# A four-layer transformer sandwich: factors summed in the transfers, the last batch by query halves, due times by kind of work

## The chip, the core and the metric

The kernel runs on one core of one Trainium2 chip. The core has TensorE (PE, matrix products, with its own queue of weight loads, PEld), VectorE (DVE), ScalarE (ACT), GpSimd (POOL) and SyncE (SP, which only issues transfers here). Each engine works through its own queue strictly in order; semaphores hold an instruction back until what it needs is there. Sixteen DMA engines move data for all queues. The metric is the device time of one execution in microseconds (us); lower is better.

## The reference, cut to what matters

The input is 8 batches of 512 tokens by 512 features, all float32. Four layers follow each other, each as `x = x + layernorm(f(layernorm(x)))`:

```
attn0:  w = softmax(x^T x)          # over features: a 512x512 Gram matrix
        f = w-weighted sum of the feature rows
ffn0:   f = sum_r (x @ factors[r]) / sqrt(8) + bias      # 8 factors of 512x512
attn1:  h = norm_scale * x / rms(x) * split_scale
        q = h Wq^T (8 heads of 64), k, v = h Wk^T, h Wv^T (2 groups)
        f = x + softmax(q k^T / 8) v  Wo^T
ffn1:   g = (x gate_w^T) * gate_s;  u = (x up_w^T) * up_s     # 1408 inner features
        f = ((silu(g) * u) down_w^T) * down_s                 # weights are -1, 0, 1
```

Because ffn0 is linear in the factors, one product with the sum of the eight factors serves for all of them.

## The kernel before, in words

**Tiles.** A batch is four token tiles of 128 rows (NT = 4); features are four blocks of 128 (KT = 4). The inner width of ffn1 is eleven tiles (NI = 11), held in two buffers hd0 and hd1 (six and five tiles, `CUTS`). Head pairs in attn1 are four (NPAIR). A 512-column float32 product is recorded as two passes, so a product over four blocks shows as eight matmul records.

**The order of work is planned.** The code of a stage does not issue instructions: it calls `add(engine, duration, function, reads, writes, ...)`, which records an operation with its data dependences, the buffers it needs and a due time `rec.prio`. `Recorder.issue` (L108) then plays a clock for each engine. Again and again it takes for each engine the operations whose inputs are there, keeps those that can start within `slack` of the earliest, picks the one with the smallest due time, and issues it. The result is a fixed order for each engine's queue. The planner gives every transfer on SP a latency of 2.6 us and the weight loads on POOL 3.0 us; a change of TensorE's tiling mode costs 0.1 us in the plan and a change of ScalarE's function table 1.3 us. Four buffers "e" hold exponentials, two "z" hold branch outputs, four "ws" attention weights, four "wgu" gate and up weights; PSUM has five banks "f" and three "g". A tag's buffers are handed on when their last reader is done.

**Due times before.** A stage's due time is batch number + a fixed offset + a span times a step: `ATTN0`, `FFN0`, `ATTN1`, `FFN1` at L1149 to L1152. One unit is one batch. So attn1 of batch b, due from b + 0.55 to b + 1.15, and ffn1, from b + 1.68, lie among the next batches' first layers, and the planner mixes them.

**Start of the kernel.** `load_fixed` (L388): for each block kt, SP loads factor 0 straight into `fsum` (L394) and the other seven into staging slots in hd0 and hd1 (L397), and DVE adds each (L401). The x of batches 0 and 1 is due earlier still (L1131). `look_at_low_bits` (L420) loads gate, up and down weights once more as raw words into the same slots, 33 pieces, and ORs them on DVE into a z buffer (L442), to see whether any low bit is set; ffn1 uses the single-pass format F32R, and a full-precision run of everything follows if the flag says so. POOL loads the down weights `wd` (L372) as soon as its queue is free.

**Layers.** Layer norms take their statistics on DVE (L495, L500), the reciprocal root on POOL (L504, L511) and the normalisation on DVE (L519); the residual add is POOL's (L537). Attn0 (L607) transposes the normalised x (L587), forms the Gram rows (L626), softmaxes them (L551 to L575) and applies them (L655). Ffn0 (L666) multiplies by fsum (L677). Attn1 (L698) forms keys, values and queries (L809, L820, L838). Then for each head pair i and query half u it forms scores for two query tiles (L869, 64-row tiling), transposes (L900, 64-row) and mixes with the values (L931, 64-column). When all pairs are done, four token tiles are projected (L959). Ffn1 (L1006) normalises all four tiles of x, splits them into a high and a low part `hl` (L990 on ACT, L999 on DVE), and for each inner tile loads the weights on POOL (L372), forms gate and up products for all 512 tokens (L1032, 8 records each), and combines them (L1052 on ACT, L1062 and L1071 on DVE). The down product (L1100) follows for each token tile, then the scale (L1113), the layer norm, the residual add and the store (L1123).

Of the kernel before, what the change touches and what calls it, by code (L numbers as in the profile page):

```python
# [12 lines left out]
I32 = mybir.dt.int32  # L13
# [40 lines left out]
class Recorder:  # L54
# [53 lines left out]
    def issue(self, places, slack=0.1):  # L108
# [26 lines left out]
        while left:  # L135
            best = None
            for e, ops in ready.items():
                able = [(s, op.prio, op.n, op) for op in ops if (s := start(op)) is not None]
                if not able:
                    continue  # L140
                first = min(able)[0]
                pick = min((p, n, s, op) for s, p, n, op in able if s <= first + slack)
                if best is None or (pick[2], pick[1]) < best[:2]:
                    best = (pick[2], pick[1], pick[3])
# [93 lines left out]
def layers(  # L238
# [99 lines left out]


# [48 lines left out]
    def load_fixed():  # L388
        rec.prio = 0.15

        slots = staging()
        for kt in range(KT):
            rec.prio = 0.15 + 0.01 * kt
            load(fsum, factors[0, ts(kt, P), :], part=kt, view=lambda t, kt=kt: t[:, kt, :])  # L394
            for r in range(1, R):
                f, j = next(slots)
                load(f, factors[r, ts(kt, P), :], part=j, view=lambda t, j=j: t[:, j, :])  # L397

                def go(f=f, j=j, kt=kt):
                    d = fsum.t[:, kt, :]  # L400
                    nc.vector.tensor_tensor(d, d, f.t[:, j, :], ALU.add)  # L401

                add("DVE", 0.69, go, reads=[(f, j)], writes=[(fsum, kt)])
        load(bias_bc, ffn_bias.partition_broadcast(P))
        rec.prio = 0.3
# [7 lines left out]
        rec.prio = 0.95  # L413
# [6 lines left out]
    def look_at_low_bits():  # L420

        low, most, total = Buf("z"), Buf("s1"), Buf("f")
        rec.prio = 1.0
        bits = lambda: low.t[:, :].bitcast(I32)
        add("DVE", 0.3, lambda: nc.vector.memset(bits(), 0), writes=[low])
        slots = staging()
        pieces = [(w, c) for w in (gate_t, up_t, down_t) for c in range(NI)]
        for n, (w, c) in enumerate(pieces):
            rec.prio = 1.0 + 0.01 * n
            raw, j = next(slots)  # L430
            if w is down_t:
                load(raw, w[ts(c, P), :], part=j, view=lambda t, j=j: t[:, j, :])
            else:
                load(
                    raw,
                    w[:, ts(c, P)].rearrange("(k p) n -> p k n", p=P),
                    part=j,
                    view=lambda t, j=j: blocks(t[:, j, :]),
                )

            def gather(raw=raw, j=j):
                nc.vector.tensor_tensor(  # L442
                    bits(), bits(), raw.t[:, j, :].bitcast(I32), ALU.bitwise_or
                )

            add("DVE", 0.69, gather, reads=[(raw, j)], writes=[low])
# [83 lines left out]
    def add_layernorm(xt, src, us=0.55):  # L530

        y = buf_of(src) if buf_of(src).tag == "z" else Buf("z")
        layernorm(whole(y), src, us)
        add(
            "POOL",
            1.27,
            lambda: nc.gpsimd.tensor_tensor(ap(xt), ap(xt), y.t[:, :], ALU.add),  # L537
# [69 lines left out]
    def stage_attn0(x, at, span):  # L607
        xn, xnT, wT = Buf("big"), Buf("big"), Buf("big")
        rec.prio = at
# [7 lines left out]
        for i in range(KT):  # L617
            rec.prio = at + span * (0.1 + 0.1 * i)
# [30 lines left out]
        for t in range(NT):  # L649
            rec.prio = at + span * (0.5 + 0.1 * t)  # L650
# [15 lines left out]
    def stage_ffn0(x, at, span):  # L666
        for t in range(NT):
            rec.prio = at + span * 0.2 * t
# [29 lines left out]
    def stage_attn1(x, at, span):  # L698
# [3 lines left out]
        for t in range(NT):  # L702
            rec.prio = at + span * 0.05 * t
# [97 lines left out]
        rec.prio = at + span * 0.2  # L801
# [28 lines left out]

        for i in range(NPAIR):
            rec.prio = at + span * (0.22 + 0.13 * i)
# [13 lines left out]
            asked = mm(pq, 3.43, queries, [wq, hT], room=[qT])  # L846
# [10 lines left out]
        wos = []  # L857
        for i in range(NPAIR):
            for u in range(2):
                aT = Buf("big")  # L860
                for s in (2 * u, 2 * u + 1):
                    rec.prio = at + span * (0.25 + 0.13 * i + 0.03 * s)
                    es = [Buf("e") for _ in range(G)]
                    scs = [Buf("f") for _ in range(G)]

                    def scores(i=i, s=s, scs=scs):
                        for g in range(G):
                            gp = ts(g, DH)
                            nc.tensor.matmul(  # L869
                                scs[g].t[:, :],  # L870
                                qT.t[gp, i, ts(s, P)],
                                kT.t[gp, :],
                                start=True,
                                stop=True,
                            )

                    add(
                        "PE",
                        0.87,
                        scores,  # L880
                        reads=[(qT, (i, u)), kT],
                        writes=scs,
                        room=[*es, aT],
                        state="64x128",
                    )
                    for g in range(G):
                        softmax_row(scs[g], es[g])


                    pts = [Buf("f") for _ in range(2)]  # L890

                    def halves(b):
                        return b.t[:, :].rearrange("p (c q) -> p c q", q=DH)

                    def transposes(es=es, pts=pts):
                        for g in range(G):
                            for t in range(NT):
                                for hf in range(2):
                                    hp = ts(hf, DH)
                                    nc.tensor.transpose(  # L900
                                        halves(pts[hf])[:, g * NT + t, :],
                                        es[g].t[hp, ts(t, P)],
                                        ident[hp, hp],
                                    )

                    add("PE", 0.56, transposes, reads=es, writes=pts, room=[aT], state="64x128")
                    for hf in range(2):

                        def place(hf=hf, s=s, aT=aT, pts=pts):
                            lo = s % 2 * P + hf * DH  # L910
                            copy = nc.scalar.copy
                            copy(columns_of(aT)[:, :, lo : lo + DH], halves(pts[hf]))  # L912

                        add(
                            "ACT",
                            0.6,
                            place,
                            reads=[pts[hf]],
                            writes=[(aT, 2 * s + hf)],
                        )  # L920
                rec.prio = at + span * (0.29 + 0.13 * i + 0.03 * s)
                po = Buf("f")

                def columns_of(b):
                    return flat(b.t).rearrange("p (c q) -> p c q", q=2 * P)

                def values_of(aT=aT, po=po):
                    for t in range(NT):
                        for g in range(G):
                            gp = ts(g, DH)  # L930
                            nc.tensor.matmul(  # L931
                                po.t[gp, : 2 * P],
                                v.t[:, t * P + g * DH : t * P + (g + 1) * DH],
                                columns_of(aT)[:, g * NT + t, :],
                                start=(t == 0),
                                stop=(t == NT - 1),
                            )

                attended = mm(po, 1.75, values_of, [aT, v], state="128x64")

                add(
                    "ACT",
                    0.4,
                    lambda i=i, u=u, po=po: nc.scalar.copy(
                        qT.t[:, i, ts(u, 2 * P)], po.t[:, : 2 * P]
                    ),
                    reads=[po],
                    writes=[(qT, (i, u))],
                )
            wos.append(Buf("ws"))  # L950
            load(wos[i], wo_t[ts(i, P), :], view=flat, after=[asked])

        for t in range(NT):
            rec.prio = at + span * (0.8 + 0.03 * t)
# [25 lines left out]
            add_layernorm(whole(x[t]), whole(z))  # L980
        return last
# [24 lines left out]
    def stage_ffn1(x, b, at, span, after):  # L1006
        PASS = 0.23 if split else 0.86
        xs = [Buf("hl") for _ in range(1 + split)]
        for t in range(NT):
            rec.prio = at + span * 0.01 * t  # L1010
            xn = Buf("row")
            mv, rstd = moments(whole(x[t]))
            normalize(whole(xn), whole(x[t]), mv, rstd, room=xs)
# [187 lines left out]
```

## Time and profile before

| | |
|---|---|
| median of 3 runs | 1568.37 us (1568.25 to 1568.81) |
| the profiled execution's own time | 1568.29 us |
| its span, first to last instruction | 1566.5 us |
| PE busy | 1503.5 us, 96% |
| PE busy in 0–117, 117–1467, 1467–1567 us | 91.6 of 117, 1333.3 of 1350, 78.7 of 100 us |
| DVE busy | 1080.4 us, 69% |
| ACT, POOL busy | 702.2 and 566.4 us |
| mean granted clock of PE | 0.988 |
| moved by DMA | 105.87 MB |

The profile is one execution, taken by the hardware profiler. "Busy" of PE counts overlapping matmuls once, and includes the draining between tiling modes; it says that PE had something in its pipe, not that it ran at its peak. In lists of instructions a line reads: start, duration, engine, source line, operation, tiles out<-in, shape, count, and in brackets the idle time before it and what ended it. In lists of groups, the numbers are total, mean of one in ns, and idle time before with its releasers.

### The profile page before, as it was taken

What the parts mean: (1) busy time and instruction counts of PE and PEld (TensorE: products, weight loads), DVE (VectorE), ACT (ScalarE), POOL (GpSimd) and SP (SyncE); (2) the same over time, 40 slices, a digit from 0 to 9 for tenths busy, and PEclk for the clock granted to TensorE, in tenths of its full rate; (3) what the DMA queues carried; (4) which work ended last, traced back from release to release, by engine and by line L of the source; (5) the groups of instructions that cost most, each with busy time, mean ns of one, the idle gap of its engine ahead of it and who ended that gap; (6) DMA issues with size and microseconds to landing.
All of it is one profiled execution on the core that took longest, in us unless ns stands there. A gap on an engine that the chain in (4) does not pass through costs nothing.

```text
span 1566.5 us, 21966 instructions
## 1 busy us (share of the span) xinstructions
PE 1503.5 (96%) x7986; PEld 923.6 (59%) x7986; DVE 1080.4 (69%) x2226; ACT 702.2 (45%) x1448; POOL 566.4 (36%) x869
## 2 busy tenths in 40 slices
PE   6799999999999999999999999999999999999896
PEld 3354456665666646665566656666566665666485
DVE  6898865679557794587845788458865678557734
ACT  2045546541376324763257523575236742277221
POOL 3614341137410473115721257103651036411532
PEclk9899999999999999999999999999999999999999
DMA  9540043212331124302142132411233102330170
GB/s 346 165 155 1 1 101 75 44 52 54 74 75 28 41 57 91 62 28 72 30 89 53 40 75 42 88 35 48 61 61 81 21 34 61 74 75 14 35 132 31
DMA packets 152471, 105.87 MB, mean 68 GB/s; under 512 B 6945, under 2 KB 132897, under 8 KB 152353
## 3 DMA queue, kind: packets, MB, share of 16 engines
q0 software_dynamic: 94512, 49.03, 16.5%
q1 hardware_dynamic: 57840, 55.34, 11.3%
q8 instruction: 65, 1.06, 0.3%
q14 instruction: 54, 0.43, 0.1%
HBM read 95.96 MB, written 8.39 MB: 67 GB/s over the span
## 4 chain that ended last, share of the span: by engine, by line
PE 81%; DVE 9%; POOL 5%; DMA 2%; issue 2%; ACT 1%; SPq 0%; POOLq 0%; ACTq 0%; DVEq 0%
PE g L1032 21%; PE g L1100 11%; PE f L869 8%; PE f L931 7%; PE f L838 7%; PE f L677 7%; PE f L900 5%; PE f L959 4%; PE f L587 3%; PE f L626 3%; DVE row L519 3%; POOL rstd L511 2%; DVE st L495 2%; PE f L820 2%; PE f L809 2%
## 5 line engine op out<-in xcount | busy, mean ns | idle before, releaser
L1032 PE MATMUL g<-hl,wgu 128*128 128x512 f32 x1408 | 350.3, 400 | 0.7 <-ACT hl L990 0.7
L551 DVE TENSOR_REDUCE s<-f 128x1 f32<-128x512 f32 x288 | 186.5, 683 | 185.3 <-PE f L869 171.3
L1032 PEld LDWEIGHTS g<-hl,wgu 128*128 128x128 f32 x1408 | 258.9, 189 | 81.5 <-issue 18.4
L504 POOL TENSOR_SCALAR ve<-mv 128x1 f32<-128x1 f32 x224 | 71.1, 317 | 523.0 <-DVE mv L500 509.0
L558 ACT ACTIVATE e<-f,s 128x512 f32<-128x512 f32 x288 | 195.8, 688 | 87.0 <-DVE s L551 81.2
L537 POOL TENSOR_TENSOR x<-x,z 128x512 f32<-128x512 f32 x128 | 169.5, 1324 | 61.6 <-DVE z L519 53.1
L1100 PE MATMUL g<-wd,hl 128*128 128x512 f32 x704 | 180.7, 406 | 3.2 <-DVE hl L999 3.2
L912 ACT COPY big<-f 128x512 f32<-128x512 f32 x256 | 134.4, 597 | 60.1 <-PE f L900 59.2
L1100 PEld LDWEIGHTS g<-wd,hl 128*128 128x128 f32 x704 | 129.0, 189 | 45.0 <-issue 11.5
L372 POOL DMA_DIRECT2D wgu<-in_up_t x88 | 67.3, 765 | 235.9 <-PE g L1032 235.8
L575 DVE TENSOR_SCALAR e<-e,s 128x512 f32<-128x512 f32 x288 | 144.0, 500 | 10.2
L511 POOL TENSOR_TENSOR rstd<-ve,mhalf 128x1 f32<-128x1 f32 x224 | 143.1, 639 | 18.1
L869 PE MATMUL f<-kv,big 64*128 64x512 f32 x512 | 138.6, 628 | 0.0
L1062 DVE SCALAR_TENSOR_TENSOR sig<-g,gs,sig 128x512 f32<-128x512 f32 x88 | 65.8, 748 | 98.4 <-ACT sig L1052 98.4
L931 PE MATMUL f<-big,kv 128*64 128x256 f32 x1024 | 124.6, 385 | 0.0
L372 POOL DMA_DIRECT2D wgu<-in_gate_t x88 | 68.7, 781 | 140.3 <-PE g L1032 137.1
L677 PE MATMUL f<-fsum,rT 128*128 128x512 f32 x256 | 116.7, 604 | 0.7 <-ACT rT L591 0.7
L959 PE MATMUL f<-ws,big 128*128 128x512 f32 x256 | 114.9, 594 | 0.6 <-ACT big L794 0.6
L838 PE MATMUL f<-big,ws 128*128 128x512 f32 x256 | 114.1, 594 | 0.0
L655 PE MATMUL f<-big,big 128*128 128x512 f32 x256 | 112.3, 594 | 0.7 <-ACT big L591 0.7
L931 PEld LDWEIGHTS f<-big,kv 128*64 128x64 f32 x1024 | 67.8, 136 | 71.8 <-ACT big L912 13.8
L900 PEld LDWEIGHTS f<-ident,e 64*128 64x128 f32 x2048 | 71.7, 139 | 43.7 <-issue 32.0
(81 smaller groups left out, 1971.3 us busy)
## 6 DMA issues: line engine op xcount, KB each, us to landing
wgu<-in_gate_t POOLq DMA_DIRECT2D x88, 256.0 KB, 3.3
wgu<-in_up_t POOLq DMA_DIRECT2D x88, 256.0 KB, 3.4
x<-in_x SPq DMA_DIRECT2D x32, 256.0 KB, 2.7
ws<-in_wq_t SPq DMA_DIRECT2D x32, 256.0 KB, 3.3
ws<-in_wo_t SPq DMA_DIRECT2D x32, 256.0 KB, 2.6
out<-x SPq DMA_DIRECT2D x32, 256.0 KB, 2.0
hd<-in_factors SPq DMA_DIRECT2D x28, 256.0 KB, 5.4
wd<-in_down_t POOLq DMA_DIRECT2D x11, 256.0 KB, 8.1
```

Of the source, the lines that this page charges most:

```text
L511: lambda: nc.gpsimd.tensor_tensor(rstd.t[:, :], ve.t[:, :], mhalf, ALU.pow),
L537: lambda: nc.gpsimd.tensor_tensor(ap(xt), ap(xt), y.t[:, :], ALU.add),
L551: lambda: nc.vector.tensor_reduce(nmax.t[:, :], sc.t[:, :], AX.X, ALU.max, negate=True),
L558: lambda: nc.scalar.activation(e.t[:, :], sc.t[:, :], AF.Exp, bias=nmax.t[:, :], accum_out=tot.t[:, :]),
L677: nc.tensor.matmul(po.t[:, :], xnT.t[:, kt, :], fsum.t[:, kt, :], start=(kt == 0), stop=(kt == KT - 1),)
L838: nc.tensor.matmul(pq.t[:, :], wq.t[:, kt, :], hT.t[:, kt, :], start=(kt == 0), stop=(kt == KT - 1),)
L869: nc.tensor.matmul(scs[g].t[:, :], qT.t[gp, i, ts(s, P)], kT.t[gp, :], start=True, stop=True,)
L900: nc.tensor.transpose(halves(pts[hf])[:, g * NT + t, :], es[g].t[hp, ts(t, P)], ident[hp, hp],)
L931: nc.tensor.matmul(po.t[gp, : 2 * P], v.t[:, t * P + g * DH : t * P + (g + 1) * DH], columns_of(aT)[:, g * NT + t, :], start=(t == 0), sto ...
L959: nc.tensor.matmul(po.t[:, :], qT.t[:, i, ts(t, P)], flat(wos[i].t), start=(i == 0), stop=(i == NPAIR - 1),)
L1032: nc.tensor.matmul(bank.t[:, :], w.t[:, kt, :], d.t[:, kt, :], start=(n == 0), stop=(n == KT * len(xs) - 1),)
L1100: nc.tensor.matmul(po.t[:, :], ap(o)[:, it - lo, :], wd.t[:, it, :], start=(it == 0 and k == 0), stop=(it == NI - 1 and k == len(ops) - 1),)
```

## The change

It has four parts.

1. *Factors.* The seven further factors of each block are no longer loaded into staging slots and added on DVE. POOL issues transfers with `accum_op=add` straight onto `fsum`. Each writes the same part of fsum as the one before, so it waits for that one's landing.
2. *Low bits.* The collector `low` is a staging slot instead of a z buffer, cleared on POOL instead of DVE, and the stage is due later (1.41 on, instead of 1.0 on).
3. *Last batch* (`EARLY = (-1,)`). Attn1 loops over query halves outside and head pairs inside, and projects a half's two token tiles when its four pairs are done. Ffn1 takes the first four inner tiles (`FEW`) for tokens 0–1, then for tokens 2–3 (each loads its weights anew, and products are 256 columns wide), and the other seven for all tokens. The residual adds of this batch's last two layers are on DVE. In every batch the down products are now recorded as after all gate and up products, and the output weights of pair i may load when the queries of pair i are done.
4. *Due times.* Every kind of operation has its own due time and steps (`DUE`), with shifts for some kinds and batches (`SHIFT`); the slack is 0.1198 instead of 0.1, and an operation that would change PE's tiling mode is ranked 0.0066 later (`STAY`).

The diff, cut to its core:

```diff
-                pick = min((p, n, s, op) for s, p, n, op in able if s <= first + slack)
+                held = state.get(e)
+                pick = min(
+                    (p + (STAY.get(e, 0.0) if op.state not in (None, held) else 0.0), n, s, op)
+                    for s, p, n, op in able
+                    if s <= first + slack
+                )
...
             for r in range(1, R):
-                f, j = next(slots)
-                load(f, factors[r, ts(kt, P), :], part=j, view=lambda t, j=j: t[:, j, :])
-
-                def go(f=f, j=j, kt=kt):
-                    d = fsum.t[:, kt, :]
-                    nc.vector.tensor_tensor(d, d, f.t[:, j, :], ALU.add)
-
-                add("DVE", 0.69, go, reads=[(f, j)], writes=[(fsum, kt)])
+
+                add(
+                    "POOL",
+                    0.8,
+                    lambda r=r, kt=kt: nc.gpsimd.dma_start(
+                        fsum.t[:, kt, :], factors[r, ts(kt, P), :], accum_op=ALU.add
+                    ),
+                    writes=[(fsum, kt)],
+                    lat=4.0,
+                )
...
-        low, most, total = Buf("z"), Buf("s1"), Buf("f")
+        most, total = Buf("s1"), Buf("f")
+        when("low", 0)
         slots = staging()
+        low = next(slots)
+        bits = lambda: low[0].t[:, low[1], :].bitcast(I32)
+        add("POOL", 0.5, lambda: nc.gpsimd.memset(bits(), 0), writes=[low])
...
+        eng, took, on = ("DVE", 0.69, nc.vector) if last else ("POOL", 1.27, nc.gpsimd)
...
+        def load_wo(i):
+            load(wos[i], wo_t[ts(i, P), :], view=flat, after=asked[i : i + 1])
+
+        if split_up:
+            for u in range(2):
+                for i in range(NPAIR):
+                    attended = attend(i, u)
+                    if u == 0:
+                        load_wo(i)
+                for t in (2 * u, 2 * u + 1):
+                    when(kinds[2], b, t % 2, u)
+                    last = project(t, attended)
+                firsts.append(last)
...
+        rounds, kind = [(every, range(NI))], "f1."
+        if b in EARLY or b - B in EARLY:
+            rounds = [((0, 1), range(FEW)), ((2, 3), range(FEW)), (every, range(FEW, NI))]
+            kind = "h1."
...
+                    sig = Buf("sig" if len(toks) == NT else "e")
+                    hd = (hds[c], lambda tt, k=it - lo, cut=cut: tt[:, k, cut])
+                    pg, pu = Buf("g"), Buf("g" if len(toks) == NT else "f")
...
-ATTN0 = (0.0, 0.163)
-FFN0 = (0.476, 0.16)
-ATTN1 = (0.55, 0.6)
-FFN1 = (1.682, 0.337)
+DUE = {
+    "x": (0.0595,),
+    "fsum": (0.0943, 0.01),
...
+    "low": (1.4104, 0.01),
+    "a0.norm": (0.0776,),
...
+    "f0": (0.3719, 0.0375),
...
+    "e1.row": (0.6591, 0.039, 0.1695, 0.0034),
...
+    "h1.gate": (1.1851, -0.0129, 0.0932),
...
+}
...
+STAY = {"PE": 0.0066}
+SLACK = 0.1198
+EARLY = (-1,)
+FEW = 4
+
+
+def due(kind, b, n, *steps):
+    first, *more = DUE[kind]
+    at = first + (b if b >= 0 else b + n) + SHIFT.get((kind[:2], b), 0.0)
+    return at + sum(k * d for k, d in zip(steps, more))
```

## The prediction

> **What bounds the kernel now.** I read first the busy shares and the forty slices of the page, then the busy time in three stretches, then TensorE's (PE's) instructions in order of time at both ends, then VectorE's (DVE's) in the first 120 us, then the transfers.
>
> ```profile
> PE 1503.5 (96%) x7986; PEld 923.6 (59%) x7986; DVE 1080.4 (69%) x2226; ACT 702.2 (45%) x1448; POOL 566.4 (36%) x869
> ...
> PE   6799999999999999999999999999999999999896
> ...
> DVE  6898865679557794587845788458865678557734
> ...
> PEclk9899999999999999999999999999999999999999
> DMA  9540043212331124302142132411233102330170
> ```
>
> PE is the bound: busy 1503.5 of 1566.5 us. It is short of nine tenths only in the first two slices and the last three. There the DMA digit or the clock digit stands out as well. The same in three stretches (columns: length, PE, weight loads, DVE, ACT, POOL busy, then clock, DMA share, GB/s):
>
> ```profile
> 0.00:117.00 117.00, 91.56 (x322) 51.11 (x323) 95.43 (x191) 30.23 (x71) 45.03 (x81) 0.94 0.69 223
> 117.00:1467.00 1350.00, 1333.28 (x7361) 814.21 (x7359) 936.79 (x1959) 654.11 (x1352) 481.55 (x734) 1.00 0.24 54
> 1467.00:1567.00 100.00, 78.70 (x308) 58.25 (x304) 48.16 (x79) 17.84 (x25) 39.86 (x54) 0.89 0.35 72
> ```
>
> PE's idle time is 25.4 us in the head, 16.7 in the 1350 us of the middle and 21.3 in the tail. No change of order can win more than these 63 us, plus what the half clock and the switches of tile mode stretch inside busy time. The gaps on PE, with what ended them in brackets:
>
> ```profile
> 8.36 4.26 PE L587 MATMUL f<-ident,big 128*128 128x128 f32 x16 [8.36 <-DVE big L519]
> ...
> 23.09 0.33 PE L624 MATMUL f<-ident,u 128*128 128x128 f32 x1 [3.14 <-ACT u L640]
> ...
> 55.35 2.12 PE L587 MATMUL f<-ident,row 128*128 128x128 f32 x8 [8.46 <-DVE row L519]
> ...
> 1467.22 10.57 PE L959 MATMUL f<-ws,big 128*128 128x512 f32 x24
> 1480.30 0.66 PE L587 MATMUL f<-ident,row 128*128 128x128 f32 x4 [2.51 <-DVE row L519]
> ...
> 1488.79 42.99 PE L1032 MATMUL g<-hl,wgu 128*128 128x512 f32 x176 [0.68 <-ACT hl L990]
> ```
>
> The 8.36 us is the first x and its layer norm. The 3.14 and 8.46 us lie behind DVE. From 1477.8 (10.57 after 1467.22) to 1488.8 PE does only 16 transposes: the last layer of the last batch waits for all four token tiles. DVE shows why the head waits:
>
> ```profile
> 16.54 0.69 DVE L401 TENSOR_TENSOR fsum<-fsum,hd 128x512 f32<-128x512 f32 x1 [4.20 <-DMA hd<-in_factors]
> ...
> 52.52 0.69 DVE L495 BATCH_NORM_STATS2 st<-x 128x6 f32<-128x512 f32 x1
> ```
>
> It stands 4.20 us in its in-order queue for a factor. It starts the layer norm of the first feed-forward layer (f0) at 52.5 us, although the first updated x left POOL at 41.8; factor adds (28 at 721 ns = 20.1 us, the last ending at 51.3) were in between. The transfers of that stretch, with the last number in us to landing:
>
> ```profile
> wgu<-in_up_t POOLq DMA_DIRECT2D x88, 256.0 KB, 3.4
> ...
> hd<-in_factors SPq DMA_DIRECT2D x28, 256.0 KB, 5.4
> wd<-in_down_t POOLq DMA_DIRECT2D x11, 256.0 KB, 8.1
> ```
>
> **What the Trainium skill says.** "Collectives: The Full Stack", section "The bandwidth ceiling", says that an add in the DMA engines costs no compute but a second source read, and halves the rate (ratio 1.93 there). The trace of before has no accumulating transfer. "DMA: Bandwidth & Descriptors", section "Rules for kernel authors", says that nothing protects the bytes between an accumulate's read and write, so the next one must wait for the semaphore of the one before; the diff's write on the same part of fsum makes that wait, and POOL stands in it. "TensorEngine Tiling (Array Packing)", section "Key Properties", says that a change of tiling mode drains the array. The trace agrees: eight records of a 512-column product take 3.43 us ahead of another full-array block and 3.53 to 3.63 ahead of a 64-row one. "TensorE: Matmul & The Clock Gate", Part 1, says that idle time drops the clock to half. The trace agrees: granted 0.53 in 50 to 60 us, and half for 13.7 us from about 1481.
>
> **The change, part by part.**
>
> *Factors by accumulating DMAs.* Removed: 28 DVE adds (20.1 us) and the waits for factors in DVE's queue (5.6 us). Also 28 issues on SP. Added: 28 issues on POOL at 0.56 (wd row) to 0.78 us (wgu row), 16 to 22 us, in a stretch where POOL is busy 45 of 117 us. They form four chains of seven, interleaved. One round of four issues takes 2.2 to 3.1 us. It must then wait for the landing, so a round lasts about one landing, and fsum is ready near 11 us (first plain load: issued behind four x loads, 6.9 us to landing) + 7 landings. Lower bound 3.4 us each (a quiet POOL load): 35 us. Upper bound 8.1 (POOL loads in the same crowded stretch): 68 us. By volume: x of two batches, fsum, biases, wd and ten raw weight pieces are 9.2 MB and the accumulates 7.3 MB; at the 346 GB/s of the first slice 48 us, with the accumulates counted twice by the skill's ratio 69 us. I take 6.4 us a landing, between the factors' 5.4 and wd's 8.1: ready at 56 us, where before the sum ended at 51.3 and f0's first product started at 57.3. Behind a waiting accumulate on POOL stand the reciprocal roots of the layer norms; DVE's normalisations wait for these, and PE for those.
>
> So f0 starts no earlier, but PE gets other work ahead of it: batch 1's first attention layer (26.5 us of products, of which before did almost nothing ahead of 57 us, for want of DVE). Of the 17.0 us of head idle after the first 8.4, I count 6 as won, and 2 for the clock no longer halved at 50 to 60: **−8**. Bounds: −16 (nearly all) and, by the slowest landing, +4.
>
> *Low-bit look.* Its collector moves from a z buffer (one of two) to a staging slot and its clearing to POOL; it is due later. The 33 gathers stay (25.0 us of DVE). In before 24 of them ran in one piece at 93.7 to 111.1 us while PE was busy with projections, so they were covered; they block softmax only if they fall elsewhere. Cost 0, between −2 and +3, inside the head's bounds.
>
> *Last batch by halves.* The order becomes half 0 over all head pairs, its two output projections, then half 1. Of the last layer, four of eleven inner tiles can run for tokens 0–1 before half 1 is done: 4 x 16 products of 256 columns, at half of 227 ns = 7.3 us. The chain from the last projection to the first product was 11.0 us; with two tiles to normalise instead of four and the residual add on DVE (690 ns for 1.26 us on POOL) I sum the rows: add 0.7, two statistics 1.7, two root pairs 1.8, two normalisations 1.1, add 0.7, transposes 0.5, split 1.3, hops 0.6 = 8.4 us. If the 7.3 us are spent ahead of the chain as filler, the gap stays 8.4 (gain 2.6 on 11.0); if kept for it, about 1 (gain 10). I take 5.5, and 2.5 for the clock. Against it: eight more weight loads. In the last stretch 22 loads now stand against some 33 us of products instead of 43, and before ran there at a DMA share of 0.71, so 0.71 x 43 / 33 = 0.92: nearly a bound of its own, +1.5. At the very end POOL's last add (1.26) becomes DVE's 0.69: −0.5. Sum **−7**, bounds −13 and +2.
>
> *Due times by kind, preference for the array's mode, wider slack.* Before, matmul records in order change mode 378 times, at about 0.1 us and more. The preference is 0.0066, while neighbouring row steps are 0.02 and tile steps 0.015 apart, so it decides few picks: perhaps one change in fifteen, 25 x 0.1 = 2.5 us. The new dues lie close to the old ones for the middle batches. I take **−2.5**, bounds −12 (most of the idle time) and +8 (another 8 us of waits on LayerNorm).
>
> Sum: −8 −7 −2.5 = −17.5 against the profiled execution's 1568.3 us (span 1566.5 and 1.8 around it; the median is 1568.4): **1551 us**.
>
> **Rivals.**
>
> *Accumulates land late* (about 7.5 to 8.3 us each). fsum is ready at 64 to 69 us and PE runs out of other work; each us costs one. Head gain 8 shrinks to 0 or −5: 1559 to 1564. For it: wd's 8.1 us and the halved rate. Against it: POOL's waits keep at most four in flight.
>
> *Accumulates become the bound: slower.* One mechanism: POOL's queue waits seven times in turn for landings. It decides from 73.5 us on, (73.5 − 11) / 7 = 8.9 us each; at 10.6 us f0 starts at 85 us and the time is 1580. For it: the raw weights' 512-byte packets crowd the same engines. Against it: no POOL load class of before averages over 8.1 us.
>
> *All three gains in full*: −16, −10, −10, so 1532. For it: the idle time exists. Against it: half of it is chain latency.
>
> *It does nothing*: the filler is used early, fsum is late by just what DVE saves; 1567.
>
> **How the numbers follow.** Forecast 0.48 (own range 1542 to 1558), late landings 0.22, full gains 0.12, slower 0.13, nothing 0.05. About 0.2%, 3 us, is what a measurement of this kernel tells from no change. Faster 0.82, same 0.05, slower 0.13. The range 1531 to 1574 leaves out about half of the full gains and most of the slower case.
>
> **What would show it.** Right: no factor adds on DVE, POOL waiting on accumulates with 5 to 8 us to landing; f0's first product at 50 to 60 us, with the transposes and first products of batch 1's first attention layer ahead of it; head idle near 18 us. In the tail a gap under 6 us after the last output projection and no half clock of 13 us there; middle idle and mode changes within a tenth of before. Wrong: f0 starting after 65 us, POOL idle for most of the first 70, a gap of 8 us or more before the last layer, or PE waiting for wgu loads in the last 40 us.

## The result and the profile after

The changed kernel takes 1638.28 us in the median (1636.45 to 1639.44), against 1568.31 for the kernel before: a ratio of 1.0446, with a 95% interval of 1.0428 to 1.0464. It is 70 us slower. 1551 was forecast.

From the page of the profile after, the busy totals of the engines and the forty slices:

```profile
PE 1501.1 (92%) x8050; PEld 928.1 (57%) x8050; DVE 1067.2 (65%) x2213; ACT 688.0 (42%) x1440; POOL 582.1 (36%) x898
...
PE   6005999999999999999999999999999999999987
...
DVE  4005998568784678567784678656784677747745
...
PEclk9556999999999999999999999999999999999998
DMA  9442500531224112421124212330134212340271
```

PE is busy for 2.4 us less than before, in a span 70.8 us longer. The whole loss is idle time, and nearly all of it lies in two and a half slices, 44 to 140 us; DVE does nothing in most of it either. By stretches (length, then busy time of PE, weight loads, DVE, ACT and POOL, clock, DMA share, GB/s):

```profile
0.00:117.00 117.00, 31.18 (x102) 17.90 (x102) 17.55 (x43) 9.91 (x20) 29.21 (x49) 0.69 0.65 138
...
1540.00:1638.00 98.00, 80.95 (x394) 62.98 (x390) 49.79 (x85) 19.51 (x31) 31.01 (x47) 0.92 0.47 93
```

PE's instructions around the gap, in order of time:

```profile
30.07 14.00 PE L668 MATMUL f<-big,big 128*128 128x512 f32 x32 [0.67 <-ACT big L604]
139.67 1.11 PE L600 MATMUL f<-ident,row 128*128 128x128 f32 x4 [95.59 <-DVE row L531]
141.45 6.73 PE L690 MATMUL f<-fsum,rT 128*128 128x512 f32 x8 [0.67 <-ACT rT L604]
```

In the kernel before the same places read:

```profile
32.89 14.00 PE L655 MATMUL f<-big,big 128*128 128x512 f32 x32 [0.68 <-ACT big L591]
57.26 8.85 PE L677 MATMUL f<-fsum,rT 128*128 128x512 f32 x16
```

PE finishes batch 0's first attention layer at 44.1 us, earlier than before (46.9). Then it stands for 95.6 us, and f0's first product is at 141.5 instead of 57.3. The waits in the first 200 us (who waited for whom: total, times, longest) give the chain of blame:

```profile
POOL fsum L407 <- DMA fsum<-in_factors: 97.6, 24, 7.1
...
DVE z L531 <- POOL rstd L523: 96.5, 6, 95.2
PE f L600 <- DVE row L531: 95.6, 1, 95.6
```

PE waits for a normalised row from DVE, DVE for a reciprocal root from POOL, and POOL, 24 times, for an accumulate to land. POOL's queue in order of time:

```profile
10.21 0.95 POOL L407 DMA_DIRECT2D fsum<-in_factors  x1
18.28 0.88 POOL L407 DMA_DIRECT2D fsum<-in_factors  x1 [7.12 <-DMA fsum<-in_factors]
...
127.32 0.87 POOL L407 DMA_DIRECT2D fsum<-in_factors  x1 [3.40 <-DMA fsum<-in_factors]
131.55 0.87 POOL L407 DMA_DIRECT2D fsum<-in_factors  x1 [3.36 <-DMA fsum<-in_factors]
132.12 0.58 POOL L516 TENSOR_SCALAR ve<-mv 128x1 f32<-128x1 f32 x1
132.79 0.57 POOL L523 TENSOR_TENSOR rstd<-ve,mhalf 128x1 f32<-128x1 f32 x1
```

Issue, wait, issue, wait: 28 accumulates in single file from 10.2 to 131.6 us, 27 steps of 4.5 us on average. Each takes 4.1 us in the median from issue to landing. The root that DVE needs stands behind all of them, at 132.8. The landing itself is shorter than the 6.4 us that I had counted with; it is the number in series that is other: 28, not seven.

Two things come together here, and no run takes them apart. The roots stand behind the file; and fsum itself is complete only when the last accumulate has landed, about 136 us by the median of 4.1. With the roots ahead of the file, f0 could not have started before that, but PE could have had batch 1's first attention layer (26.5 us of products by the prediction's count) in the gap.

The order comes from the planner. In `issue`, a successor on the same engine counts as ready 0.05 us after the first one's end, whatever latency was given; `lat` counts only for successors on other engines and for the time at which buffers come free:

```
o.ready = max(o.ready, at + op.dur + self.OWN if o.eng == e else end)
```

For arithmetic that is close to the trace: the root at 132.79 starts 0.09 us after the end of the step that it needs (132.12 and 0.58). For a transfer that waits for a transfer issued by the same engine, the plan believes in 0.85 us (0.8 for the issue and 0.05) where 4.5 pass. So it saw no reason to interleave the four blocks: it took block 0's seven accumulates, then block 1's, in order of due time, all ahead of the roots, and planned 24 us (28 x 0.85) for what takes 122.

### The profile page after: what moved, and what is told of

It is laid out like the page before. It is cut to its first block, busy times and chain, and to the rows that moved or that the text cites. A ratio compares the mean times of both kernels' runs of the same rounds, so it can differ in the third digit from the quotient of the medians.

```text
span 1637.3 us, 22053 instructions
## 1 busy us (share of the span) xinstructions
PE 1501.1 (92%) x8050; PEld 928.1 (57%) x8050; DVE 1067.2 (65%) x2213; ACT 688.0 (42%) x1440; POOL 582.1 (36%) x898
## 4 chain that ended last, share of the span: by engine, by line
PE 72%; POOL 9%; DVE 9%; DMA 5%; issue 4%; ACT 0%; POOLq 0%; SPq 0%; DVEq 0%
PE g L1091 16%; PE g L1159 11%; PE f L881 8%; PE f L943 7%; PE f L852 7%; PE f L969 5%; PE f L912 5%; DMA fsum<-in_factors 5%; PE f L668 3%; PE f L639 3%; POOL rstd L523 3%; POOL x L550 2%; DVE row L531 2%; PE f L600 2%; DVE st L507 2%
## 5 line engine op out<-in xcount | busy, mean ns | idle before, releaser
L1091 PE MATMUL g<-hl,wgu 128*128 128x512 f32 (+1 forms) x1408 | 343.7, 396 | 3.0 <-DVE sig L1121 1.1
L516 POOL TENSOR_SCALAR ve<-mv 128x1 f32<-128x1 f32 x224 | 67.7, 303 | 558.9 <-DVE mv L512 531.8
L550 POOL TENSOR_TENSOR x<-x,z 128x512 f32<-128x512 f32 x120 | 158.5, 1321 | 58.7 <-DVE z L531 42.3
L588 DVE TENSOR_SCALAR e<-e,s 128x512 f32<-128x512 f32 x288 | 153.6, 533 | 10.2
L600 PE MATMUL f<-ident,row 128*128 128x128 f32 x384 | 56.2, 280 | 103.7 <-DVE row L531 102.3
L881 PE MATMUL f<-kv,big 64*128 64x512 f32 x512 | 132.7, 620 | 0.2 <-ACT big L924 0.2
L381 POOL DMA_DIRECT2D wgu<-in_gate_t x92 | 72.5, 788 | 162.6 <-PE g L1091 161.2
L604 ACT COPY rT<-f 128x512 f32<-128x512 f32 x32 | 18.5, 588 | 250.3 <-PE f L600 250.3
L381 POOL DMA_DIRECT2D wgu<-in_up_t x92 | 71.0, 772 | 135.7 <-PE g L1091 130.5
L600 PEld LDWEIGHTS f<-ident,row 128*128 128x128 f32 x384 | 44.0, 142 | 131.4 <-DVE row L531 111.1
```

The source lines that it names most:

```text
L381: lambda: nc.gpsimd.dma_start(view(buf.t), src),
L550: lambda: on.tensor_tensor(ap(xt), ap(xt), y.t[:, :], ALU.add),
L588: lambda: nc.vector.tensor_scalar(e.t[:, :], e.t[:, :], rtot.t[:, :], None, ALU.mult),
L881: nc.tensor.matmul(scs[g].t[:, :], qT.t[gp, i, ts(s, P)], kT.t[gp, :], start=True, stop=True,)
L1091: nc.tensor.matmul(bank.t[:, cut], w.t[:, kt, :], d.t[:, kt, cut], start=(n == 0), stop=(n == KT * len(xs) - 1),)
```

## The experiments

Theory S: the single file of accumulates on POOL, with the roots behind it, is the whole loss. Rivals: V, accumulating transfers are slow by volume; R, the halves or the due times lose time of their own. In the diffs, unless said otherwise, the changed kernel is the base.

**The accumulates and the rest of the change apart.** First, all but the accumulates:

```diff
-                add("POOL", 0.8, lambda r=r, kt=kt: nc.gpsimd.dma_start(
-                        fsum.t[:, kt, :], factors[r, ts(kt, P), :], accum_op=ALU.add), ...)
+                f, j = next(slots)
+                load(f, factors[r, ts(kt, P), :], part=j, view=lambda t, j=j: t[:, j, :])
+                add("DVE", 0.69, go, reads=[(f, j)], writes=[(fsum, kt)])
```

> The changed kernel with the factors summed as before (loads into staging slots, adds on DVE); all else of the change stays. Theory S (the 28 accumulates are landed one at a time in POOL's queue, and the layer norms' roots stand behind them; that is the whole loss): f0's first product comes back from 141.5 to about 57 us, so 1638 - 84 = about 1554 us. Rival V (accumulating transfers are slow by volume): the same 1554. Rival R (the halves or the due times lose time of their own): above 1575.

Measured: 1556.18 us, ratio 0.992 (0.9897 to 0.9943), with f0's first product back where it was:

```profile
57.30 6.03 PE L688 MATMUL f<-fsum,rT 128*128 128x512 f32 x8 [0.68 <-ACT rT L602]
```

Then the accumulates alone, put into the kernel before by the opposite edit:

> The kernel before with only the factors' accumulating transfers; old due times, no halves. S: its planned POOL queue also has 25 accumulates in one piece, block by block, and 3 more after the first root; f0's first product near 140 us instead of 57, so 1568 + 84 = about 1650 us. V: the same. R: well below 1638, since the loss would need the other parts.

Measured: 1654.31 us, ratio 1.0542 (1.0522 to 1.0561). The accumulates cost 82.1 us taken out of the changed kernel (1638.28 − 1556.18) and 86.8 put into the one before. R is out: everything else in the change is a gain of some 11 us (1567.50 − 1556.18). S and V both fit so far.

**The same accumulates, four in flight.** Two ways: recorded round by round, or with the planner's rule mended.

```diff
-            for r in range(1, R):          # inside the loop over kt, due by kt
+        for r in range(1, R):
+            for kt in range(KT):
+                when("fsum", 0)
```

> The changed kernel with the same 28 accumulates recorded round by round (all four blocks of factor 1, then of factor 2, and so on) at one due time, so that four are in flight on POOL instead of one. Volume, count and place in the queue are unchanged. S: seven waits of about 4 to 5 us instead of 28, POOL free near 45 us, f0's first product near 50 to 55 us, total about 1550 us. V: fsum is complete no earlier than 120 us and the total stays above 1620.

Measured: 1588.07 us, ratio 1.0121 (1.0104 to 1.0138).

```diff
-                o.ready = max(o.ready, at + op.dur + self.OWN if o.eng == e else end)
+                own = o.eng == e and op.lat < 1.0
+                o.ready = max(o.ready, at + op.dur + self.OWN if own else end)
```

> The changed kernel with one rule of the planner altered: an operation that depends on a transfer of its own engine becomes ready when the transfer has landed, not 0.05 us after its issue. The plan then puts other POOL work between rounds of four accumulates. S: as with the rounds, or a few us better because roots are not behind 28 issues: about 1545 us. V: above 1620.

Measured: 1572.96 us, ratio 1.0027 (1.0017 to 1.0038). With the same 28 transfers and the same bytes, the order alone gives back 50 and 65 us; that is what S says. V in its strong form (no better than 1620) is out, but S's numbers are missed too, by 38 and 28 us. Something else shows once the file is gone. In the waits of the first 120 us of the version by rounds:

```profile
DVE st L509 <- DMA x<-in_x: 41.2, 9, 29.2
...
POOL fsum L409 <- DMA fsum<-in_factors: 25.1, 25, 2.3
```

POOL now waits little each time. But DVE stands up to 29.2 us for an x, which is that of batch 2. SP's queue (start, duration, then the transfer) shows why it is late:

```profile
16.91 29.78 SPq L360 DMA_DIRECT2D hd<-in_gate_t  x10
46.73 5.07 SPq L360 DMA_DIRECT2D x<-in_x  x3
```

Ten raw weight loads, whose issue takes 10 us in the changed kernel, take SP 29.8 us here, and land after 16.4 us in the median. The x stands behind them. Full DMA engines alone don't explain the slow issue: their share is 1.13 in 17 to 47 us here, and 1.14 in 16 to 26 us of the changed kernel, where the issue takes 10. What differs is that four accumulates are in flight instead of one; how they slow SP was not traced.

**How much one accumulate in the file costs.**

```diff
-            for r in range(1, R):
+            for r in range(1, 5):
```

> The changed kernel with four further factors per block added instead of seven: 16 accumulates instead of 28, still one after the other; the last three factors are left out of the sum, so the output is another. S (28 landings in series, 4.4 us from issue to next issue): 12 x 4.4 = 53 us less than the changed kernel, about 1585 us. V (volume): the accumulates moved 7.3 MB in 122 us, far under the engines' rate, so 12 fewer would save at most 12 x 0.76 = 9 us (256 KB at 346 GB/s): about 1629 us.

Measured: 1599.54 us, ratio 1.0205 (1.0186 to 1.0223): 38.7 us less than the changed kernel, not 53. The file itself shortens as expected: the last issue comes at 77.2 us instead of 131.6, 54 us for 12 accumulates, 4.5 each. But the plan came out otherwise around it. POOL's stall now begins before batch 0's softmax is through, so the 14 us of context products, which the changed kernel has done before its gap, come after it, and f0 starts at 105.6, 28 us after the last issue instead of 10. Far above V's 9 us either way.

**What bounds the interleaved sum.** On the version with the landing rule, first only the order on SP:

```diff
     ("x", 1): 0.0585,
+    ("x", 2): -0.7,
```

> The kernel with the landing rule, and the x of batch 2 due 0.7 earlier, so that its three loads stand ahead of the ten raw weight loads on SP instead of behind them. Theory Q (what is left of the head's loss there is DVE standing for this x behind SP's raw loads, 21 us at the longest): the wait goes and the time falls from 1573 to about 1560 us. Rival C (the DMA engines are full, share 1.0 and more up to 80 us, whatever the order on SP): no more than 4 us won, about 1570.

Measured: 1563.36 us, ratio 0.997 (0.9963 to 0.9978). That is 9.6 us of the 13 that Q gave, and more than the 4 that C allowed: DVE's waits for x in the first 120 us fall from 29.2 us to 12.0. f0's first product moves from 85.3 to 75.4, still 18 us later than with DVE adds. Then the raw loads held back as well (with that they come after batch 2's x too):

```diff
+        for buf in (...):           # hd0 and hd1
+            add("POOL", 0.15, lambda buf=buf: nc.gpsimd.memset(buf.t[:, :, 0:1], 0),
+                writes=[(buf, j) for j in range(n)], after=summed_up)
```

> The kernel with the landing rule, and the raw weight loads held back until POOL is through with the accumulates (a one-column clear of the staging slots on POOL, which the loads then have to wait for). Q: about 1560, as with x first. C (accumulates and raw loads share full engines): a round of four accumulates shortens from about 7 to 4 or 5 us, fsum is complete near 48 us, f0's first product comes at 55 to 60 us, and the time is about 1550 us, under the version with DVE adds (1556).

Measured: 1553.5 us, ratio 0.9905 (0.9886 to 0.9924). So 9.9 us more than the order alone: C has its part. But f0's first product is at 71.3, not at 55 to 60, and the last accumulate is issued at 59.0, one in 1.8 us. The gain over DVE adds, 2.7 us, is within what the two intervals leave open. The busy time of the engines in ten-us stretches of this version, with DMA share and GB/s at the end:

```profile
40.00:50.00 10.00, 10.00 (x32) 5.23 (x31) 3.76 (x9) 3.32 (x8) 6.12 (x10) 1.00 1.10 209
50.00:60.00 10.00, 8.02 (x25) 3.79 (x23) 3.65 (x8) 1.07 (x2) 7.93 (x13) 1.00 0.98 158
```

From 50 to 60 us, where no other large transfer is issued, the DMA engines are full at 158 GB/s. The kernel before moved 364 GB/s in 20 to 40 us:

```profile
20.00:40.00 20.00, 14.64 (x57) 9.35 (x58) 17.84 (x33) 6.27 (x15) 1.55 (x2) 0.91 1.01 364
```

Engine time per byte is (0.98 / 158) / (1.01 / 364) = 2.2 times as long with accumulates. Whether that rate or the latency of each landing holds the sum back was then tried with plain loads in the same places:

```diff
-                        fsum.t[:, kt, :], factors[r, ts(kt, P), :], accum_op=ALU.add
+                        fsum.t[:, kt, :], factors[r, ts(kt, P), :]
```

> The version with raw loads held back, its 28 accumulates turned into plain loads of the same size, place and waits on POOL; the addition is left out, so fsum holds the last factor only. Theory A (an accumulate keeps the DMA engines busy about twice as long as a plain load, and that rate bounds the sum even with four in flight): from 1.72 us a transfer (48 us for 28) to POOL's own issue time of 0.87, 24 us for 28; f0's first product before 60 us instead of 71, and about 1543 us instead of 1553. Rival L (latency, not rate: each landing simply takes 6.5 us): the 28 still take over 40 us and the time stays within 3 us of 1553.

Measured: 1540.79 us, ratio 0.9824 (0.9807 to 0.984), 12.7 us under the version it came from, f0's first product at 58.4. A holds for the time. Its 24 us for the 28 is missed: they take 35.8 (issues from 11.3 to 47.1). POOL waits for landings only 6.4 us of it; the plan, made for accumulates, keeps other POOL work between the rounds. Landing falls from 6.5 to 3.9 us. The next two stretches are of this version:

```profile
30.00:40.00 10.00, 10.00 (x36) 5.52 (x35) 4.03 (x11) 3.97 (x10) 7.07 (x15) 1.00 0.92 288
40.00:50.00 10.00, 10.00 (x24) 4.38 (x23) 6.24 (x14) 0.00 (x0) 9.27 (x18) 1.00 0.71 250
```

The engines carry 288 GB/s at 0.92, and PE has no gap there. This run alone doesn't part rate from latency, since a plain load has less of both. A stretch of the changed kernel, in which one accumulate at a time is all that moves, does more:

```profile
60.00:120.00 60.00, 0.00 (x0) 0.00 (x0) 0.00 (x0) 0.00 (x0) 13.16 (x15) 0.50 0.47 64
```

One accumulate in flight takes 0.47 of the engines at 64 GB/s; four fill them (0.98) at 158. So the rate sets a floor for any order: at 158 GB/s the 28 (7.3 MB) need about 46 us, an estimate from these figures.

**Half of the blocks each way**, on the version with x first (blocks 0 and 2 by DVE adds, edit as in the first experiment):

> The version with the landing rule and x first, with blocks 0 and 2 of the factors summed on DVE as before and blocks 1 and 3 by accumulates, two in flight. A: the engines' extra work halves (14 accumulates), DVE keeps 10 us of adds, the sum is complete near 45 us; about 1548 us, a few us under both the DVE adds (1556) and the held raw loads (1553). Rival B (whatever the sum costs, DVE's in-order waits for factors come back): 1555 or more.

Measured: 1558.2 us, ratio 0.9948 (0.9931 to 0.9965). The number is as rival B has it. DVE's waits for factors are back in full, 6.1 us where the version with DVE adds for all blocks has 5.2, but that one starts f0 at 57.3 and this one at 72.7. Here POOL stands 26.3 us in eight waits of up to 8.3, and it issues its last accumulate at 68.4. The longest wait comes before the first accumulate: block 1's plain load of factor 0 stands behind block 0's seven factors on SP, so the chains start at 21.4 us instead of 10.8. The run is thus no clean test of two chains against four.

**The other two parts**, on the version with DVE adds. Without the halves (`EARLY = ()`):

> The changed kernel with DVE adds, and the last batch in whole order again (no query halves, no half-token tiles; its residual adds stay on DVE). Theory H (the halves pay only what the loss in the tail shows, 25.1 us beside 27.2 before): 2 us more than with DVE adds and halves, 1558 us. Rival G (the halves give what was forecast, 7 us): 1563 us or more.

Measured: 1564.03 us, ratio 0.9976 (0.9968 to 0.9985). The halves are worth 7.9 us, so G is right and H, my reading of the tail's idle sum after the result, is wrong. PE's instructions without halves:

```profile
1463.22 10.57 PE L967 MATMUL f<-ws,big 128*128 128x512 f32 x24
1480.36 2.12 PE L598 MATMUL f<-ident,row 128*128 128x128 f32 x8 [6.57 <-DVE row L529]
...
1487.77 42.76 PE L1089 MATMUL g<-hl,wgu 128*128 128x512 f32 x176 [0.68 <-ACT hl L1030]
```

and with them:

```profile
1470.54 3.60 PE L967 MATMUL f<-ws,big 128*128 128x512 f32 x8
...
1478.84 1.18 PE L1089 MATMUL g<-hl,wgu 128*128 128x256 f32 x8 [0.87 <-DMA wgu<-in_gate_t]
1480.09 1.22 PE L1089 MATMUL f<-hl,wgu 128*128 128x256 f32 x8
1482.64 0.66 PE L598 MATMUL f<-ident,row 128*128 128x128 f32 x4 [1.33 <-DVE row L529]
...
1485.28 0.53 PE L1089 MATMUL g<-hl,wgu 128*128 128x256 f32 x1 [0.68 <-ACT hl L1030]
```

Half-token products stand where PE had 6.57 us of nothing, and the clock stays up: 0.96 over 1450 to 1490 with halves, 0.82 without. Between the two profiles PE's idle time differs by 5.7 us and its busy time by 4.0, and in the tail PE waits 1.4 us for gate weights with halves. H compared sums of idle time over stretches that did not hold the same work.

Without the preference for the current tiling mode:

```diff
-STAY = {"PE": 0.0066}
+STAY = {}
```

> The changed kernel with DVE adds, without the preference for the array's current tiling mode. By the forecast (one change of mode in fifteen, 0.1 us each): 2.5 us more, 1558.7 us. Rival: nothing, 1556.2 within 1.5 us, and what the due times gain comes from the dues themselves.

Measured: 1593.99 us, ratio 1.0167 (1.015 to 1.0184), 37.8 us slower than with it. Neither expectation is near. It isn't the switches: matmul records change mode 363 times without the preference and 356 times with it. The waits of PE in 800 to 1400 us, without it:

```profile
PE f L910 <- DVE e L586: 8.3, 6, 1.8
PE f L598 <- DVE row L529: 7.5, 6, 1.5
PE f L635 <- ACT u L651: 5.4, 3, 2.6
```

PE waits for softmax and layer norm 27 us in that stretch, against 2.8 us with it. Over the whole span, which is 36.9 us longer, 26.1 us are idle time of PE and 10.8 us are longer busy time (1513.8 for 1503.0); the second part wasn't followed up. My reading is that a small term in the ranking has led the plan down another path, with batches meeting in another phase. Which pick was the first to go astray wasn't traced, and whether any other small change of these due times would cost as much was not tried.

## Why the prediction was wrong, point by point

**The accumulates: the step that failed.** I wrote that the 28 issues "form four chains of seven, interleaved", and that fsum is ready near 11 us plus seven landings. They stand in one file of 28, the last is issued at 131.6 us where I had the sum ready at 56, and the head is 82 us longer than with DVE adds instead of 8 shorter than before. I gave no reason for "interleaved". It needs a planner that counts the landing between two accumulates of a block, and the line of `issue` that leaves it out stood in the kernel before. The interleaved order, tried by mending the rule, gives 1573 us, 17 us more than DVE adds (1572.96 − 1556.18), so my number for this step (−8) would have failed too, by a smaller amount.

The second mis-sized term was the time until fsum is ready in that order: I set 56 us between 48 (accumulates counted once) and 69 (twice), and it is the upper end. With x first the last accumulate is issued at 62.7 us and lands near 70. (In the mended plan it is issued at 70.6, after 8.7 us in which POOL stands for DVE.) The Trainium skill's ratio for an add in the DMA engines ("Collectives: The Full Stack", section "The bandwidth ceiling", 1.93 between two collectives) is near what is measured here, 2.2 by share and rate. A landing with four in flight takes 6.5 to 7.7 us in the median, near the 6.4 I chose or above it.

Two of the signs that I had named for "wrong" came true: f0 after 65 us, and POOL idle for most of the first 70.

**"Behind a waiting accumulate on POOL stand the reciprocal roots"** was right, and is the way in which the loss reached PE. It should have been followed to its end: in POOL's in-order queue the root at 132.8 us waited for all 28 accumulates.

**The slower rival** had the mechanism (POOL waiting in turn for landings) with the wrong count, seven. It asked for 8.9 us a landing or more, and at 10.6 it had f0 at 85 us. In the event 4.1 us a landing and 28 in series put f0 at 141.5 us. I gave this rival 0.13, and the range ended below it.

**The halves: right in the sum, with one term off.** −7 was forecast, −7.9 measured. The chain from the last projection to the first product for tokens 2–3 takes 11.1 us (1474.14 to 1485.28) and not the 8.4 that I summed. That is no shorter than in the kernel before (11.0), and 2.9 us less than in the version without halves (14.0). What pays is the filler: six half-token products lie in the chain, so PE idles 3.5 us in it instead of 9.6, and the clock stays up. That is in the range between "spent ahead" and "kept for it" from which I took 5.5.

**Due times: right in the sum, wrong in the reason.** −2.5 was forecast for them. Without halves and with DVE adds the kernel is 3.8 us under the one before (1564.03 and 1567.85), with the moved low-bit look and the shorter last add (−0.5) in it. The carrier is another than I had it. Without halves the changes of mode fall from 378 to 365, 1.3 us at the 0.1 of the forecast, and with halves the preference accounts for 7 of them (363 and 356); yet the kernel without it is 37.8 us slower, so the preference acts through the order of the plan. What the due times would give in a plan that was not made with it stays open.

**The low-bit look: not free beside accumulates.** Cost 0 was given with "covered by projections" as its reason, and only DVE's gathers were priced there; the ten early raw loads stood in the volume of the factors' sum alone. With four accumulates in flight its raw loads are worth another 9.9 us, by the version that holds them back. What they cost in the changed kernel itself was not measured.

The parts +82.1, −7.9 and −3.8 give 70.4 us for the 70.0 measured. They add up by construction, since each is the step from one version to the next.

## What to carry to other kernels

When a plan or a code order is what puts instructions on a queue, read how it treats a dependence between two operations of the same queue; here a transfer's issue took 0.9 us and its landing 4.1, and the in-order engine that waited for landings held back everything behind it. Count what stands in series, not what could run side by side. Moving sums into accumulating transfers took 20 us of work off DVE but cost the DMA engines 2.2 times the time per byte. At the start of this kernel, where their share was 0.99 and 1.01 in the first 40 us even before the change, that gave nothing that could be told from DVE adds (1553.5 and 1556.2 us at best). It may pay where the engines are idle; no run tried that.

## What the runs showed that was not expected

- Plain loads in place of the accumulates, in the same queue positions, are 12.7 us faster, though the work of PE and DVE is the same: the DMA engines are full at 158 GB/s with accumulates and at 364 GB/s with plain loads.
- SP's issue of other loads was slow beside accumulates: ten raw loads took 29.8 us to issue with four in flight and 10.2 us with one, at DMA shares of 1.13 and 1.14; eleven took 8.4 us after the accumulates were through.
- Taking a ranking term of 0.0066 out of this plan costs 37.8 us, with the count of mode changes practically unchanged.
- Of the versions that compute the whole layer stack, the one with the landing rule and held raw loads is the fastest at 1553.5 us, and the one with DVE adds and the rest of the change takes 1556.2; both are faster than the kernel before (ratios 0.9905 and 0.992), and the runs do not tell them apart.
